# Queries and keys on two column halves and a first image projected between products, in place of a rearranged tail

## The chip, the core and the metric

The kernel runs on one core of one Trainium2 chip. The metric is the device time of one execution in microseconds. Time before the change: 3698.84 us, the median of three runs (3698.0 to 3699.41). The span in the profile, from the first to the last instruction, is 3696.3 us; the granted TensorE clock averages 0.994.

## The reference, cut to what matters

```python
# layer 0: attention over the 4096 pixels of each of 4 images, 256 channels, 32 for q and k
x = inputs.reshape(B, N, Cin)                 # B, N = 4, 4096
q = x @ Wq + bq;  k = x @ Wk + bk             # 32 columns each
v = x @ Wv + bv                               # 256 columns
attn = softmax(einsum('bnd,bmd->bnm', q, k))
x = gamma * einsum('bnm,bmc->bnc', attn, v) + inputs
# layer 1: depthwise 3x3 convolution to 768 channels, two pointwise products, a residual ...
perceived = depthwise_conv3x3(x, w_perc) + b_perc          # 256 -> 3*256
hid = gelu(w_up1 . perceived + b_up1)                      # 768 -> 512
h = x + w_up2 . hid + b_up2                                # 512 -> 256
# ... and attention of each pixel over its 3x3 neighbourhood
out = h + local_attention(h, w_qkv, b_qkv)
```

All of it is fp32.

## The kernel before

The image is cut into blocks of 512 pixels: 8 blocks an image, 32 slots in all. In slot `s` block `s` goes through the softmax's weights and products of layer 0. Between them stand the convolution of block `s - 2` on VectorE (`perceive`), the pointwise products of block `s - 3` (`hidden`, `update`, `local_values`) and the local attention of block `s - 5`. When the slots are over, a tail finishes the last blocks.

Projections. `staged[s]` holds x of block `s`; `wqk2` holds the 64 columns of queries and keys twice, to make 128:

```python
def project_qk(s):
    xc = staged[s]
    ps = bank("m", f"qk_{s}")                                  # one of 2 PSUM banks
    for kin in range(CH):                                      # CH = 2 halves of 256 channels
        nc.tensor.matmul(ps, lhsT=wqk2[:, kin]..., rhs=xc[:, kin, :], start=..., stop=...)
    st = tile_of([P, NB], "st", f"st_{s}")                     # 1 buffer
    nc.scalar.activation(st, ps, AF.Identity, bias=bqk2)
    keys[s] = tile_of([P, P], "ka", f"ka_{s}", NBLK + 1)
    for j in range(GRP):                                       # 4 key groups to 4 row quarters
        nc.sync.dma_start(out=keys[s][j * CQK : (j + 1) * CQK, :], in_=st[CQK : 2 * CQK, bass.ts(j, P)])
    nc.sync.dma_start(out=packed[:, bass.ts(s, NB)], in_=st[:CQK, :])   # queries to DRAM

def project_v(s, pair): ...            # 4 matmuls of 256 columns, bias on VectorE; two calls a block
def spread_queries(s): ...             # four copies of block s's queries from DRAM to the 4 row quarters (qa)
def energy(s, G): ...                  # four matmuls with 32 rows each, on four row quarters (L221)
def weight(s, G, half): ...            # exponential on ScalarE
def product(s, G, half): ...           # four matmuls into acc (L240)
```

The start: all eight blocks of the first image are projected ahead of the first energy.

```python
for s in range(2):
    fetch(s)                           # x of a block: two loads of 256 KB on SyncE's queue
# ... wv, bv, gam and all weights of layer 1 are loaded on ScalarE's queue ...
for s in range(NBLK):
    for job in projections(s):         # qk, v, v
        job()
    if s + 2 < NBLK:
        fetch(s + 2)
spread_queries(0)
energy(0, 0); weight(0, 0, 0); weight(0, 0, 1)
```

For images 2 to 4 the projections stand in the last slot of the image before: one block's jobs after every second product.

The convolution on VectorE: for each of 6 channel groups a first tap on ScalarE and 8 steps on VectorE (L320), in `perceive(s, parts)`; a part may be fewer rows than a block, and for the last two blocks the next part's first tap is given out one part ahead. The tail before:

```python
# in slot 31, from the 5th point on:
extra = perceive(30, [(i, 0, RB - 1) for i in range(NPC // 2)])    # 7 of 8 rows, 3 of 6 groups
# after slot 31:
turns[:] = ["m", "e", "acc", "m", "acc"]                            # PSUM banks in turn
conv = chain(perceive(30, [(i, RB - 1, RB) for i in range(NPC // 2)] + whole[NPC // 2 :]),
             perceive(31, whole))
for k in range(29, 32):
    ...                                # hid with 6 steps after each, other jobs with 0, 1, 2 or 3;
                                       # local attention of k - 2 and, already begun, of k - 1
```

For the last two blocks VectorE takes over what GpSimd does for the others: the multiplication by `near`, the local sum, and the last addition, which goes to a tile of its own:

```python
engine = nc.vector if s >= NSLOT - 2 else nc.gpsimd
...
o = tile_of([P, NB], "lo", f"lo_{s}_{c}", 2)
nc.vector.tensor_tensor(o, ps, lrdens[s], ALU.mult)
watch(o)                               # GpSimd adds it to `watched`
engine, res = nc.gpsimd, o
if s >= NSLOT - 2:
    engine, res = nc.vector, tile_of([P, NB], "o", f"res_{s}_{c}", 2)
engine.tensor_tensor(rv, ov, pixels(s, c), ALU.add)
nc.sync.dma_start(out=out[b, :, c, bass.ts(g, NB)], in_=res)
```

`hidden` is L339, `update` L365 with its `h` on VectorE L371, `guide` L439, `local_values` L479, `scores` L516, `border` L462, `local_denominator` L571 with its reciprocal L573, `local_product` L582.

Of the kernel before, what the change touches and what calls it, by code (L numbers as in the profile page):

```python
# [27 lines left out]
KR, KW = 4, W // 2  # L28
QW = KW + 1
# [15 lines left out]
def attention_then_perception_kernel(  # L45
# [34 lines left out]
    def unshifted():  # L80
# [14 lines left out]
        def job_bank(name):  # L95
            turns.append(turns.pop(0))
            if turns[-1] == "e":
                return psum.tile([P, GRP, NB], F32, tag="e", name=name, bufs=1)[:, 0, :]
            return bank(turns[-1], name)

        wqk2 = pool.tile([P, CH, 2, 2, CQK], F32, tag="wqk2", name="wqk2")
        bqk2 = pool.tile([P, 1], F32, tag="bqk2", name="bqk2")
        for r in range(2):
            nc.scalar.dma_start(out=wqk2[:, :, r], in_=w_qk)
            for s in range(2):
                at = (2 * r + s) * CQK
                nc.scalar.dma_start(out=bqk2[at : at + CQK, :], in_=b_qk[:, s : s + 1])
# [39 lines left out]
        def fetch(s):  # L149
            b, g = divmod(s, NBLK)  # L150
            staged[s] = tile_of([P, CH, NB], "xc", f"xc_{s}", 2)
            rows = x[b].rearrange("p c (h w) -> p c h w", w=WP)
            for c in range(CH):
                nc.sync.dma_start(
                    out=staged[s][:, c, :].rearrange("p (h w) -> p h w", w=W),
                    in_=rows[:, c, 1 + g * RB : 1 + (g + 1) * RB, 1 : 1 + W],
                )

        def project_qk(s):
            xc = staged[s]  # L160
            ps = bank("m", f"qk_{s}")
            for kin in range(CH):
                nc.tensor.matmul(  # L163
                    ps, lhsT=wqk2[:, kin].rearrange("p r s d -> p (r s d)"),
                    rhs=xc[:, kin, :], start=(kin == 0), stop=(kin == CH - 1),
                )
            st = tile_of([P, NB], "st", f"st_{s}")
            nc.scalar.activation(st, ps, AF.Identity, bias=bqk2)
            keys[s] = tile_of([P, P], "ka", f"ka_{s}", NBLK + 1)
            for j in range(GRP):  # L170
                nc.sync.dma_start(  # L171
                    out=keys[s][j * CQK : (j + 1) * CQK, :],
                    in_=st[CQK : 2 * CQK, bass.ts(j, P)],
                )
            nc.sync.dma_start(out=packed[:, bass.ts(s, NB)], in_=st[:CQK, :])
# [20 lines left out]
        def projections(s):  # L196
            return [
                lambda: project_qk(s),
                lambda: project_v(s, 0),
                lambda: project_v(s, 1),  # L200
            ]
# [82 lines left out]
        HALO = KR // 2  # L284
# [6 lines left out]
        def perceive(s, parts):  # L291

            g = s % NBLK
            ahead = s >= NSLOT - LAG_PERC
            percs.setdefault(s, {})

            def first(i, r0, r1):
                if i not in percs[s]:
                    if not ahead:
                        perc = tile_of([P, NB], "perc", f"perc_{s}_{i}", NPERC)  # L300
                    else:

                        if i % 2 == 0:
                            percs[s, i] = spare(f"perc_{s}_{i}")
                        perc = percs[s, i - i % 2][:, i % 2, :]
                    percs[s][i] = perc
                tap_of(i, r0, r1, 0)

            def tap_of(i, r0, r1, tap):
                half, j = divmod(i, MULT)  # L310
                dy, dx = divmod(tap, 3)
                acc = percs[s][i].rearrange("p (h w) -> p h w", w=W)[:, r0:r1, :]
                win = xv[:, half, g * RB + dy + r0 : g * RB + dy + r1, dx : dx + W]
                wt = wperc[:, half, j, tap : tap + 1]
                if tap == 0:
                    nc.scalar.activation(  # L316
                        acc, win, AF.Identity, bias=bperc[:, half, j : j + 1], scale=wt
                    )
                else:
                    nc.vector.scalar_tensor_tensor(acc, win, wt, acc, ALU.mult, ALU.add)  # L320

            for n, part in enumerate(parts):
                if n == 0 or not ahead:
                    first(*part)
                if ahead and n + 1 < len(parts):
                    first(*parts[n + 1])
                for tap in range(1, TAPS):
                    tap_of(*part, tap)
                    if part[2] - part[1] > 1 or tap % 4 == 0:
                        yield  # L330

        whole = [(i, 0, RB) for i in range(NPC)]
# [177 lines left out]
        def scores(s, half):  # L510
# [19 lines left out]
            engine = nc.vector if s >= NSLOT - 2 else nc.gpsimd  # L530
            engine.tensor_tensor(  # L531
# [8 lines left out]
        def local_sum(s):  # L540
# [5 lines left out]
            engine = nc.vector if s >= NSLOT - 2 else nc.gpsimd  # L546
            engine.memset(t, 0.0)
            for half in range(2):
                for _, rows, at in pieces(s):
                    to = tv[:, rows, columns(half)]  # L550
                    p = near_ws[s, half][:, at].rearrange("p (h w) -> p h w", w=QW)
                    engine.tensor_tensor(to, to, p, ALU.add)
# [23 lines left out]
        def local_product(s, c):  # L576
# [14 lines left out]
            engine, res = nc.gpsimd, o  # L591
            if s >= NSLOT - 2:
                engine, res = nc.vector, tile_of([P, NB], "o", f"res_{s}_{c}", 2)
            ov, rv = (t.rearrange("p (h a w) -> p h a w", a=2, w=KW) for t in (o, res))
            engine.tensor_tensor(rv, ov, pixels(s, c), ALU.add)
            nc.sync.dma_start(out=out[b, :, c, bass.ts(g, NB)], in_=res)
# [22 lines left out]
        for s in range(2):  # L619
            fetch(s)  # L620
        wv = loaded(w_v, "wv")
        bv = loaded(b_v.partition_broadcast(P), "bv", [P, C])
        gam = loaded(gamma.partition_broadcast(P), "gam", [P, 1])
        wperc = loaded(w_perc, "wperc")
# [9 lines left out]

        for s in range(NBLK):
            for job in projections(s):
                job()
            if s + 2 < NBLK:
                fetch(s + 2)
        spread_queries(0)  # L640
        energy(0, 0)
        weight(0, 0, 0)
        weight(0, 0, 1)
        points = 2 * NG
        for slot in range(NSLOT):
# [19 lines left out]
            conv = perceive(slot - LAG_PERC, whole) if slot >= LAG_PERC else iter(())  # L665
            n_steps, stepped = NPC * (TAPS - 1), 0
            extra, begun = iter(()), 4
            if slot == NSLOT - 1:

                extra = perceive(slot - 1, [(i, 0, RB - 1) for i in range(NPC // 2)])  # L670
            done = 0
            for point in range(points):
# [25 lines left out]
                while stepped < min(n_steps, -(-(point + 1) * n_steps // (points - 2))):  # L698
                    next(conv, None)
                    stepped += 1  # L700
                    if point >= begun and stepped % 3:
                        next(extra, None)
                if nxt and half == 1:
                    for job in nxt[G]:
                        job()
                    if G + 2 < NBLK:
                        fetch(slot + 1 + G + 2)
            for _ in chain(conv, extra):
                pass
# [3 lines left out]
        turns[:] = ["m", "e", "acc", "m", "acc"]  # L713
        conv = chain(
            perceive(
                NSLOT - 2,
                [(i, RB - 1, RB) for i in range(NPC // 2)] + whole[NPC // 2 :],
            ),
            perceive(NSLOT - 1, whole),
        )  # L720

        def run(*jobs):
            for job, steps in jobs:
                job()
                for _ in range(steps):
                    next(conv, None)

        last = NSLOT - 1
        for k in range(NSLOT - LAG_HID, NSLOT):
            hid, upd, new = hidden_jobs(k)  # L730
            g0, g1, s0, s1, bd, ls, ld, l0, l1 = attention_jobs(k - 2)
            hid = [(job, 6) for job in hid]
            if k == last:
                for _ in conv:
                    pass
            if k == NSLOT - LAG_HID:
                run(
                    (g0, 1), hid[0], (g1, 1), hid[1], (s0, 1), hid[2], (s1, 1), (bd, 0), (ls, 0),
                    hid[3], (upd[0], 3), (ld, 0), (upd[1], 2),
                )  # L740
            else:
                run(
                    hid[0], (ld, 0), hid[1], (l0, 1), hid[2], (l1, 1), hid[3],
                    (upd[0], 3), (upd[1], 2),
                )
            g0, g1, s0, s1, bd, ls = attention_jobs(k - 1)[:6]
            run((g0, 1), (g1, 1))
            if k == NSLOT - LAG_HID:
                run((l0, 1), (l1, 1))
            run(*((job, 1) for job in new), (s0, 1), (s1, 1), (bd, 0), (ls, 0))  # L750
        ld, l0, l1 = attention_jobs(last - 1)[6:]
        att = attention_jobs(last)
        below(NSLOT)
        local_values(NSLOT, 0)
        for job in (*att[:2], ld, *att[2:6], l0, l1, *att[6:]):
            job()

        test = [tile_of([P, NB], "o", f"test_{i}", 2) for i in range(2)]
        nc.vector.tensor_scalar(test[0], watched, -WATCH_MAX, None, ALU.is_ge)
        nc.vector.scalar_tensor_tensor(  # L760
            test[1], watched, WATCH_MAX, test[0], ALU.is_le, ALU.mult
        )
        good = tile_of([P, 1], "good", "good")
# [400 lines left out]
```

## Time and profile before

| | |
|---|---|
| time, median of 3 | 3698.84 us |
| span of the profile | 3696.3 us |
| first energy, first product | 56.2 us, 63.5 us |
| end of slot 0 (its denominator on TensorE) | 128.1 us |
| denominator of slot 31 | 3508.05 us |
| last comparison | 3688.85 us |
| matmul records of products / hid / e / qk | 4096 / 1536 / 2048 / 128 |

Each row of a timeline or of a group gives the engine, the line of the kernel, the operation, the tiles as out<-in, and a count. Matmul lengths overlap because the engine is pipelined: where records follow closely, the distance from start to start is what each costs. What stands in brackets is the time the engine sat idle before the row and what ended it. A logical fp32 matmul appears as two records. PE is TensorE, PEld its weight loads, DVE VectorE, ACT ScalarE, POOL GpSimd, SP SyncE; a q after the name is the engine's instruction queue.

### The profile page before, as it was taken

Reading aid. Unit: us, or ns where it says so; the run is one execution under the profiler, and the core shown is the slowest. Engines: PE = TensorE matmul, PEld = TensorE weight load, DVE = VectorE, ACT = ScalarE, POOL = GpSimd, SP = SyncE. Lnnn points to the kernel's source line nnn. Section 1 sums busy time; section 2 is a strip of 40 time slices with the busy share of each in tenths; the row PEclk is TensorE's granted clock in tenths of the full one; section 3 lists DMA queues with packets and bytes.
Section 4 is the critical chain, followed back from the end, with each engine's and each line's share of the span. In section 5 each row is a group of like instructions: output and inputs, shape, how many; then the busy total and the mean of one; then the engine's idle time right before and its main releaser. Section 6 shows DMA issues by size and latency. Waiting matters only on the chain.

```text
span 3696.3 us, 29966 instructions
## 1 busy us (share of the span) xinstructions
PE 3642.3 (99%) x11598; PEld 1741.6 (47%) x11598; DVE 2451.4 (66%) x2716; ACT 1166.2 (32%) x1302; POOL 744.9 (20%) x735
## 2 busy tenths in 40 slices
PE   8999999999999999999999999999999999999997
PEld 4334444454444444455444444445544444444445
DVE  2376656756677776666666777765676666777794
ACT  1223333223333333332333333333233333333231
POOL 1000012111212222112212222221122212222242
PEclk9999999999999999999999999999999999999999
DMA  4000000110000000021000000001100000000000
GB/s 108 15 18 9 3 0 15 37 39 11 15 15 15 15 15 4 11 45 42 15 1 15 15 15 15 15 19 37 32 15 15 3 12 15 15 15 12 6 12 19
DMA packets 101592, 69.05 MB, mean 19 GB/s; under 512 B 74432, under 2 KB 79552, under 8 KB 101312
## 3 DMA queue, kind: packets, MB, share of 16 engines
q1 hardware_dynamic: 98304, 63.47, 6.6%
q10 hardware_dynamic: 3136, 3.58, 0.3%
q8 instruction: 93, 1.52, 0.2%
q14 instruction: 59, 0.48, 0.0%
HBM read 46.04 MB, written 18.87 MB: 18 GB/s over the span
## 4 chain that ended last, share of the span: by engine, by line
PE 94%; DVE 3%; DMA 1%; POOL 1%; SPq 0%; issue 0%; ACT 0%; ACTq 0%; DVEq 0%; POOLq 0%
PE acc L240 47%; PE hid L339 18%; PE e L221 7%; PE dx L365 6%; PE lv L479 3%; PE g L439 3%; PE lo L582 2%; PE s L516 2%; PE v L184 2%; DVE perc L320 2%; PE qk L163 1%; PE dps L263 1%; PE ld L571 1%; SPq L171 0%; DMA packed<-st 0%; DVE lrden L573 0%
## 5 line engine op out<-in xcount | busy, mean ns | idle before, releaser
L240 PE MATMUL acc<-p,v 128*128 128x512 f32 x4096 | 1841.5, 595 | 3.2 <-DVE o L269 3.2
L320 DVE SCALAR_TENSOR_TENSOR perc<-xp,wperc,perc 128x512 f32<-128x512 f32 (+2 forms) x1560 | 1315.6, 849 | 624.3 <-ACT perc L316 590.3
L240 PEld LDWEIGHTS acc<-p,v 128*128 128x128 f32 x4096 | 769.9, 191 | 915.2 <-issue 901.4
L229 ACT ACTIVATE p<-e 128x1024 f32<-128x1024 f32 x512 | 524.4, 1024 | 1573.5 <-PE e L221 744.6
L339 PE MATMUL hid<-perc,wup 128*128 128x512 f32 x1536 | 694.1, 601 | 0.0
L254 DVE TENSOR_TENSOR den<-den,p 128x1024 f32<-128x1024 f32 x480 | 594.2, 1238 | 74.2 <-ACT p L229 68.2
L339 PEld LDWEIGHTS hid<-perc,wup 128*128 128x128 f32 x1536 | 282.5, 190 | 398.1 <-issue 390.9
L531 POOL TENSOR_TENSOR lp<-lp,near 128x396 f32<-128x396 f32 x60 | 87.0, 1452 | 1352.4 <-ACT lp L529 1352.4
L221 PE MATMUL e<-qa,ka 32*128 32x512 f32 x2048 | 295.0, 642 | 5.1 <-DMA qa<-packed 3.1
L365 PE MATMUL dx<-hid,wup 128*128 128x512 f32 x512 | 235.9, 604 | 0.0
L229 ACT ACT_TABLE_LOAD x116 | 148.8, 1283 | 233.8 <-issue 119.2
L343 ACT ACTIVATE hid<-hid,bup 128x512 f32<-128x512 f32 x128 | 88.0, 687 | 397.7 <-PE hid L339 397.7
L265 DVE RECIPROCAL rden<-dps 128x512 f32<-128x512 f32 x32 | 107.4, 3358 | 118.0 <-PE dps L263 118.0
L371 DVE SCALAR_TENSOR_TENSOR h<-dx,bup,xp 128x256 f32<-128x256 f32 x128 | 55.9, 478 | 187.4 <-PE dx L365 187.4
L143 POOL TENSOR_TENSOR watched<-watched,lrden 128x512 f32<-128x512 f32 x32 | 62.3, 1948 | 527.9 <-DVE lrden L573 527.9
L143 POOL TENSOR_TENSOR watched<-watched,lo 128x512 f32<-128x512 f32 x64 | 131.2, 2051 | 181.1 <-DVE lo L589 174.8
L221 PEld LDWEIGHTS e<-qa,ka 32*128 32x128 f32 x2048 | 81.0, 183 | 173.8 <-issue 162.9
L343 ACT ACT_TABLE_LOAD x121 | 155.2, 1283 | 11.9 <-PE hid L339 9.7
L365 PEld LDWEIGHTS dx<-hid,wup 128*128 128x128 f32 x512 | 92.5, 189 | 138.7 <-issue 114.8
L316 ACT ACTIVATE perc<-xp,bperc,wperc 128x512 f32<-128x512 f32 (+2 forms) x195 | 154.9, 798 | 0.0
L143 POOL TENSOR_TENSOR watched<-watched,den 128x512 f32<-128x512 f32 x32 | 40.6, 1269 | 507.0 <-DVE den L256 507.0
L189 DVE TENSOR_TENSOR v<-v,bv 128x512 f32<-128x512 f32 x64 | 44.0, 691 | 130.9 <-PE v L184 130.6
(87 smaller groups left out, 2227.7 us busy)
## 6 DMA issues: line engine op xcount, KB each, us to landing
xp<-in_x SPq DMA_DIRECT2D x32, 528.0 KB, 4.7
xc<-in_x SPq DMA_DIRECT2D x64, 256.0 KB, 3.9
out<-lo SPq DMA_DIRECT2D x60, 256.0 KB, 2.0
qa<-packed SPq DMA_DIRECT2D x128, 64.0 KB, 3.7
ka<-st SPq DMA_DIRECT2D x128, 16.0 KB, 1.8
packed<-st SPq DMA_DIRECT2D x32, 64.0 KB, 1.9
wup<-in_w_up ACTq DMA_DIRECT2D x1, 1536.0 KB, 7.3
out<-res SPq DMA_DIRECT2D x4, 256.0 KB, 2.0
```

Source lines behind the costliest of these rows:

```text
L143: nc.gpsimd.tensor_tensor(watched, watched, values, ALU.add)
L221: nc.tensor.matmul(e[:, j, :], lhsT=key[rows, :], rhs=queries[s][rows, :], start=True, stop=True,)
L229: nc.scalar.activation(p, energies[s, G][:, 2 * half : 2 * half + 2, :], AF.Exp)
L240: nc.tensor.matmul(accs[s][c], lhsT=v[:, 2 * half + i, bass.ts(c, P)], rhs=p[:, i, :], start=(first and i == 0), stop=(G == NG - 1 and hal ...
L254: nc.vector.tensor_tensor(den, den, p, ALU.add)
L316: nc.scalar.activation(acc, win, AF.Identity, bias=bperc[:, half, j : j + 1], scale=wt)
L320: nc.vector.scalar_tensor_tensor(acc, win, wt, acc, ALU.mult, ALU.add)
L339: nc.tensor.matmul(ps, lhsT=wup1[:, i, bass.ts(d, P)], rhs=percs[s][i], start=(i == 0), stop=(i == NPC - 1),)
L343: nc.scalar.activation(hids[s][:, d, :], ps, AF.Gelu, bias=bup1[:, d : d + 1])
L365: nc.tensor.matmul(ps, lhsT=wup2[:, d, bass.ts(c, P)], rhs=hids[s][:, d, :], start=(d == 0), stop=(d == NHC - 1),)
L439: nc.tensor.matmul(ps, lhsT=wg[:, kin, bass.ts(i, P)], rhs=pixels(s, kin), start=(kin == 0), stop=(kin == CH - 1),)
L479: nc.tensor.matmul(ps[:, half * C : (half + 1) * C], lhsT=keys_of(s, t, half, kin), rhs=wlv[:, kin, :], start=(kin == 0), stop=(kin == CH ...
```

## The change

It has three parts.

1. Queries and keys of two blocks are computed at once: block `s` on the lower 64 columns of TensorE, block `s + 1` on the upper 64. This is to replace the doubled columns by useful ones.
2. The first image's projections mostly move between the products of slot 0, as those of the other images stand already; x of blocks 2 to 7 is loaded at the start on ScalarE's queue, into buffers that are free at that time, and the weights of layer 1 are loaded after that. This is to let the products begin sooner.
3. The tail is another: the convolution is done block by block with four steps after each job, no part of it stands in slot 31, and GpSimd does its usual work for the last two blocks as well, except the last addition, which VectorE does in place.

```diff
-        wqk2 = pool.tile([P, CH, 2, 2, CQK], F32, tag="wqk2", name="wqk2")
+        wqk = pool.tile([P, CH, 2, CQK], F32, tag="wqk", name="wqk")
         def fetch(s):
-            staged[s] = tile_of([P, CH, NB], "xc", f"xc_{s}", 2)
+            # blocks 2..7 of the first image: in "hid", "h" and "lq" buffers; others as before
+            queue = nc.scalar if 2 <= s < NBLK else nc.sync
         def project_qk(s):
             for kin in range(CH):
-                nc.tensor.matmul(
-                    ps, lhsT=wqk2[:, kin].rearrange("p r s d -> p (r s d)"),
-                    rhs=xc[:, kin, :], start=(kin == 0), stop=(kin == CH - 1),
-                )
+                for r in range(2):
+                    nc.tensor.matmul(
+                        ps[2 * r * CQK : 2 * (r + 1) * CQK, :],
+                        lhsT=wqk[:, kin].rearrange("p s d -> p (s d)"),
+                        rhs=staged[s + r][:, kin, :], start=(kin == 0), stop=(kin == CH - 1),
+                    )
             # one activation to st; then packed and ka of block s, and of block s + 1
         def projections(s):
+            pair = [lambda: project_qk(s)] if s % 2 == 0 else []
+            return pair + [lambda: project_v(s, 0), lambda: project_v(s, 1)]
 ...
+        for s in range(NBLK):
+            fetch(s)
         gam = loaded(gamma.partition_broadcast(P), "gam", [P, 1])
+        first = {s: projections(s) for s in range(NBLK)}
+        first[0].pop(0)()
+        spread_queries(0)
         # the weights of layer 1 are loaded here
-        for s in range(NBLK):
-            for job in projections(s):
-                job()
-            if s + 2 < NBLK:
-                fetch(s + 2)
-        spread_queries(0)
+        for job in first[0] + first[1]:
+            job()
+        first[2].pop(0)()
         energy(0, 0)
         weight(0, 0, 0)
         weight(0, 0, 1)
+        first = [first[4][:1] + first[2], first[3], first[6][:1] + first[4][1:], first[5], first[6][1:], first[7]]
 ...
+            if slot == 0:
+                nxt = first + [[]] * (NG - len(first))
-            if slot == NSLOT - 1:
-                extra = perceive(slot - 1, [(i, 0, RB - 1) for i in range(NPC // 2)])
 ...
-            engine = nc.vector if s >= NSLOT - 2 else nc.gpsimd      # near, local sum
+            nc.gpsimd. ...
-            if s >= NSLOT - 2:
-                engine, res = nc.vector, tile_of([P, NB], "o", f"res_{s}_{c}", 2)
+            last = nc.vector if s >= NSLOT - 2 else nc.gpsimd
+            last.tensor_tensor(ov, ov, pixels(s, c), ALU.add)
 ...
-        turns[:] = ["m", "e", "acc", "m", "acc"]
-        # (the loop of the tail before)
+        turns.append("acc")
         for k in range(NSLOT - LAG_HID, NSLOT):
             hid, upd, new = hidden_jobs(k)
+            att = attention_jobs(k - LAG_ATT + LAG_HID)
+            ahead = k + LAG_HID - LAG_PERC
+            conv = perceive(ahead) if ahead < NSLOT else iter(())
+            for job in (
+                att[0], hid[0], att[1], hid[1], att[2], hid[2], att[3], att[4], att[5],
+                hid[3], att[6], *upd, att[7], att[8], *new,
+            ):
+                job()
+                for _ in range(4):
+                    next(conv, None)
+        att, last = (attention_jobs(a) for a in (NSLOT - 2, NSLOT - 1))
         below(NSLOT)
         local_values(NSLOT, 0)
-        for job in (*att[:2], ld, *att[2:6], l0, l1, *att[6:]):
+        for job in (*att[:6], *last[:6], att[6], last[6], *att[7:], *last[7:]):
             job()
```

`attention_jobs` gives guide, guide, scores, scores, border, local sum, local denominator, product, product. The final test of `watched` is written with four VectorE operations instead of three.

## The prediction

> **What bounds the kernel now.** I read the page first: busy shares, then the chain of waits.
>
> ```profile
> PE 3642.3 (99%) x11598; PEld 1741.6 (47%) x11598; DVE 2451.4 (66%) x2716; ACT 1166.2 (32%) x1302; POOL 744.9 (20%) x735
> ...
> PE 94%; DVE 3%; DMA 1%; POOL 1%; SPq 0%; issue 0%; ACT 0%; ACTq 0%; DVEq 0%; POOLq 0%
> ```
>
> TensorE is busy nearly throughout and carries 94% of the chain. So in the middle of the run a microsecond of TensorE removed is a microsecond of time, and work moved to other engines is free. The 3% of VectorE and 1% of DMA must lie where TensorE waits, so I asked for TensorE's timeline at both ends, and at one slot that projects the next image.
>
> The slot first. The columns are start, length, engine, line, operation, count; a logical fp32 matmul is two records, and the distance between starts is its cost on the path.
>
> ```profile
> 704.87 1.88 PE L163 MATMUL qk<-xc,wqk 128*128 128x512 f32 x4
> 706.59 3.62 PE L184 MATMUL v<-wv,xc 128*128 128x256 f32 x16
> 710.13 1.14 PE L221 MATMUL e<-qa,ka 32*128 32x512 f32 x8
> 711.21 5.42 PE L339 MATMUL hid<-perc,wup 128*128 128x512 f32 x12
> ```
>
> One block's queries and keys cost 706.59 - 704.87 = 1.72 us, its values 3.54 us, one group of four energies 1.08 us, and nothing waits in between.
>
> The start:
>
> ```profile
> 49.53 3.62 PE L184 MATMUL v<-wv,xc 128*128 128x256 f32 x16
> 56.23 3.23 PE L221 MATMUL e<-qa,ka 32*128 32x512 f32 x8 [3.08 <-DMA qa<-packed]
> 61.49 2.09 PE L221 MATMUL e<-qa,ka 32*128 32x512 f32 x8 [2.03 <-ACT p L229]
> 63.51 7.79 PE L240 MATMUL acc<-p,v 128*128 128x512 f32 x16
> ...
> 128.09 1.02 PE L263 MATMUL dps<-den,ones 128*128 128x512 f32 x2
> ```
>
> The first product starts at 63.5 us, after all eight blocks of projections and two bare waits; slot 0 then takes 128.1 - 63.5 = 64.6 us without a gap. The projections before it are worth 8 x (1.72 + 3.5) = about 42 us, so some 21 us of these 63.5 are filling and waiting. SyncE and ScalarE say what the filling is made of:
>
> ```profile
> 0.81 5.62 SPq L154 DMA_DIRECT2D xc<-in_x  x4
> 18.66 0.69 ACT L168 ACTIVATE st<-qk,bqk 128x512 f32<-128x512 f32 x1 [5.27 <-DMA packed<-st]
> ```
>
> Four quarter-megabyte loads of x took 5.6 us to issue, 1.4 us each, though the same pair takes 1.02 us later, when nothing else is in flight: issuing is held back while the transfers crowd. And `st` has one buffer, so its next writing waits for the copies out of it.
>
> The end:
>
> ```profile
> 3508.05 1.25 PE L263 MATMUL dps<-den,ones 128*128 128x512 f32 x2 [2.16 <-DVE den L256]
> ...
> 3572.33 2.07 PE L571 MATMUL ld<-lsum,ones 128*128 128x512 f32 x2 [6.46 <-POOL lsum L557]
> 3574.19 6.81 PE L339 MATMUL hid<-perc,wup 128*128 128x512 f32 x12
> ...
> 3688.10 0.56 PE L766 MATMUL good_sum<-good,ones 128*128 128x1 f32 x2 [6.53 <-DVE good L764]
> ```
>
> The tail lasts from 3509 to 3688.9 us (the last comparison), 180 us, and 7.4 us of the span follow it. Its TensorE work, by starts, is 42 us for each of three blocks (hid 20.6, dx 6.9, g 3.4, s 3.1, lo 3.1, lv 3.5, ld 0.9, border 0.3) and 11 us for each of two more blocks of local attention: 150 us. So the present tail is already within 30 us of TensorE's own work.
>
> **What the skill says.** The Trainium skill's "TensorE: Matmul & The Clock Gate", section "Part 3: Packing small matmuls", says that matmuls on different row or column tiles of the array run at once, and gives 2.38x for three column tiles. The trace agrees for row tiles: the records of four energies start 7 ns apart, and the group costs 1.08 us where four matmuls of that length in a row would cost 3.4 us. No run here has column tiles yet. "TensorEngine Tiling (Array Packing)", section "Tiling Modes", says that a change of tiling mode drains the array. The trace fits: from a product's last record to the first energy record pass 0.52 us, against 0.43 between two products. "DMA: Bandwidth & Descriptors", section "Issuing engines are not separate DMA queues", says that loads issued by ScalarE share the engines with SyncE's; so twelve loads moved to ScalarE's queue should not arrive sooner. No trace before tests this. The clock-gate page's Part 1 says that an idle array drops to half clock: after the 6.46 us wait above, twelve records of hid took 6.81 us instead of 5.42.
>
> **Part 1: queries and keys of two blocks at once.** Before, the 128 columns held the 64 wanted ones twice; a pair of blocks costs 2 x 1.72 = 3.44 us. After, four logical matmuls of 64 columns stand on two halves. If the halves overlap as rows do, four half-steps of 0.43 us remain, with about 0.1 us for each that the energies also lose (0.53 instead of 0.43 from pass to pass): 1.8 to 2.2 us, I take 2.1. Gain 1.34 us a pair, 5.4 us an image. For images 2 to 4 this lies wholly on TensorE's path: **-16 us**. The halved count of `st` activations (0.69 us each) is off the path.
>
> **Part 2: the first image.** Only queries and keys of blocks 0 to 3 and values of 0 and 1 stay ahead of the first product; 6 x 3.5 + 2 x 2.1 = 25 us move into slot 0. The slot then ends at (first product) + 64.6 + 25. For the first product: x of blocks 0 and 1 has landed at about 9 us (issued by 6.4, and 3 us or more to landing). But ScalarE now issues twelve more loads of x before its first `st`, and at 1.4 us each (they meet the same crowd) it comes free at about 19 to 21 us, against 11.4 before. The `st` ends at 21 to 22; SyncE then issues ten copies and four of `qa` at about 0.58 us each, 8 us, and the last lands 2 to 3 us later: energies at about 32, exponentials, first product at about 35 (estimates from those rows). The slot ends at 124 to 125 instead of 128.1. Were ScalarE not held up, the product would start near 29 and the gain be 10. I take **-5 us**, which holds the first image's share of Part 1.
>
> **Part 3: the old tail.** It drops three things: half of one block's convolution inside slot 31, the unbroken row of convolution steps, and VectorE doing GpSimd's work for the last two blocks. Each job is followed by four steps, so 40 steps stand before the local denominator's reciprocal, and the next block's `lv` follows the last `h`. A step takes 0.86 us (1315.6 us over 1560 is 0.84, more when GpSimd works alongside).
> - Block 29: VectorE leaves slot 31 at 3517.5. 40 x 0.86 + 3.4 (reciprocal) + 4 x 0.86 + 0.9 (`h`) + 4 x 0.86 + 0.9 = 46.4, so 3564, and 3568 after `lv`.
> - Block 30: 1 us to start, 3 us of waiting for first taps that ScalarE holds behind its TensorE results (estimate), 46.4, `lv` 3.5: 3622.
> - Block 31 has no steps: 27.6 us of TensorE to the last hid, 4.3 for the local sum (9.8 us from scores to denominator at 3542.5, of which 5.5 are covered), then 0.9 + 6.9 + 3.1 + 3.5, and 1 us of cold clock: 3669.
> - The last two attentions: values 1.7, twice (3.4 + 3.1 + 0.3 + 1.2 waiting): 3687. GpSimd needs about 8 more for the second sum: 3695. Denominator and reciprocal 5: 3700. Then four results in turn, each product 0.7, watched by GpSimd 1.5 (the addition in place must wait for that), added 0.8: 3712. Test and end 4: 3716, plus the 7.4: 3723 against 3696.3.
>
> That is **+27 us**. Sum: -16 - 5 + 27 = +6, so 3698.8 + 6 = **3705 us**.
>
> **The rivals.** (a) Column halves don't overlap: two streams of 128 rows each must be read at once, which row tiles never asked. Then Part 1 brings nothing and the time is about 3724. The skill's table speaks against it; no record here does. (b) The tail costs much less, because VectorE still has slack: in it only blocks 29 and 30 exceed TensorE's 42 us, and 0.77 us a step (seen where GpSimd is idle) saves 4 us in each. With a smoother end the tail is +15 and the time 3692. For it: the before tail's own gaps; against it: VectorE is the chain from 3465 to 3556 even now. (c) The start gains its full 10 to 12 us, with the others as predicted: 3699. (d) The start becomes DMA-bound, as weights and x crowd the small copies: the first product at 42 us, 3712.
>
> **Range and chances.** Part 1 may lie between 0 and -18, Part 2 between +2 and -12, Part 3 between +15 and +38; they are independent, so 8 times in 10 the sum lies between -11 and +25: 3688 to 3724. Two per cent is 74 us, beyond any of these: within 2% is nearly certain.
>
> **What would show it.** qk at slot 7: about 2.1 us to the next start for every second block, four records of 64 columns in pairs some ns apart; 3.4 us would prove rival (a). The first L240 near 35 us and slot 0's dps near 125. ScalarE's first `st` after 19 us, or near 12 if issue isn't held. In the tail: dps to dps shows slot 31 unchanged at 107.7 us, `lv` of blocks 29 and 30 waiting for VectorE, spacing about 54 us, and the last four results with GpSimd between VectorE's steps. The prediction is wrong if the tail grows under 15 us or the start loses time.

## The result and the profile after

The changed kernel takes 3712.92 us (median of six runs, 3710.0 to 3714.57) against 3698.7: a ratio of 1.0037, with a 95% interval of 1.0024 to 1.005. It is 14 us slower; 3705 was predicted, in a range of 3688 to 3724. In the two profiles the spans differ by 3707.9 - 3696.3 = 11.6 us, and all that follows divides these.

The page of the changed kernel, its busy shares and its chain:

```profile
PE 3629.5 (98%) x11598; PEld 1726.9 (47%) x11598; DVE 2434.1 (66%) x2676; ACT 1159.9 (31%) x1287; POOL 750.1 (20%) x753
...
PE 95%; DVE 2%; DMA 1%; POOL 1%; issue 0%; ACTq 0%; ACT 0%; SPq 0%; POOLq 0%; DVEq 0%
```

TensorE's busy time went down by 12.8 us and the span went up: the loss lies where TensorE waits. In the rows that follow, `qk` and `v` are the projections of layer 0, `e` its energies, `acc` its products and `dps` the denominator that ends a slot; `ld`, `lv` and `lo` are denominator, values and products of the local attention. TensorE's timeline in slot 7, where the second image is projected:

```profile
707.48 3.60 PE L253 MATMUL acc<-p,v 128*128 128x512 f32 x8
711.01 1.94 PE L176 MATMUL qk<-xc,wqk 128*64 128x512 f32 x8
712.88 3.72 PE L200 MATMUL v<-wv,xc 128*128 128x256 f32 x16
716.53 1.14 PE L234 MATMUL e<-qa,ka 32*128 32x512 f32 x8
...
809.12 1.81 PE L576 MATMUL lo<-lp,lv 128*128 128x99 f32 x12 [1.08 <-DVE v L205]
```

Two blocks' queries and keys take 712.88 - 711.01 = 1.87 us. They are eight records of 64 columns now, in the time of little more than four. The last row is a wait that the slot did not have before. The start, TensorE first, then ScalarE and SyncE:

```profile
26.24 1.94 PE L176 MATMUL qk<-xc,wqk 128*64 128x512 f32 x8 [0.78 <-DVE v L205]
35.47 3.13 PE L234 MATMUL e<-qa,ka 32*128 32x512 f32 x8 [7.29 <-DMA qa<-packed]
40.63 2.09 PE L234 MATMUL e<-qa,ka 32*128 32x512 f32 x8 [2.03 <-ACT p L242]
42.65 7.67 PE L253 MATMUL acc<-p,v 128*128 128x512 f32 x16
...
131.96 1.02 PE L276 MATMUL dps<-den,ones 128*128 128x512 f32 x2
```

```profile
5.00 15.38 ACTq L166 DMA_DIRECT2D xc<-in_x  x12
21.60 1.28 ACT L182 ACT_TABLE_LOAD   x1 [21.60 <-DMA xc<-in_x]
22.89 0.69 ACT L182 ACTIVATE st<-qk,bqk 128x512 f32<-128x512 f32 x1
...
26.70 0.58 SPq L186 DMA_DIRECT2D packed<-st  x1
29.57 2.42 SPq L188 DMA_DIRECT2D ka<-st  x4
```

The first product starts 21 us sooner than before, but 25 us of projections moved behind it, so slot 0 ends at 131.96, which is 3.9 us later. ScalarE spends 15.38 us issuing the loads of x and reaches its first `st` at 22.89 us. The issue goes at the pace of the transfers: the DMA engines move about 217 GB/s in this time, and at this rate twelve loads of 256 KB take 14.5 us (an estimate). The tail:

```profile
3498.78 1.02 PE L276 MATMUL dps<-den,ones 128*128 128x512 f32 x2
...
3536.23 2.08 PE L565 MATMUL ld<-lsum,ones 128*128 128x512 f32 x2 [4.19 <-POOL lsum L551]
3538.09 9.19 PE L361 MATMUL dx<-hid,wup 128*128 128x512 f32 x16
...
3554.48 3.29 PE L475 MATMUL lv<-wlv,h 128*128 128x256 f32 x14 [2.66 <-DVE h L367]
...
3701.00 0.56 PE L727 MATMUL good_sum<-good,ones 128*128 128x2 f32 x2 [9.99 <-DVE good L725]
```

In each of blocks 29 and 30 TensorE waits in two places: for GpSimd's local sum ahead of `ld`, and for VectorE's `h` ahead of `lv`. After the first of these waits the clock granted to TensorE is half for a while (a mean of 0.76 from 3538.1 to 3547.1), and the sixteen records of dx take 9.19 us; without a wait they take 7.03.

From denominator to denominator on TensorE's timeline, and from the last of them to the end of the span:

| stretch, us | before | after | difference |
|---|---|---|---|
| start to the end of slot 0 | 128.09 | 131.96 | +3.9 |
| slot 1 | 80.63 | 82.81 | +2.2 |
| slots 7, 15 and 23, together | 447.2 | 434.2 | -13.0 |
| slot 31 | 108.76 | 106.43 | -2.3 |
| tail | 188.25 | 209.12 | +20.9 |
| all other slots | | | 0.0 |

Unrounded, the sum is 11.6 us. Slot 1 has the same instructions in both kernels; what its 2.2 us are is said with the last experiment.

### The profile page after: what moved, and what is told of

Read it like the earlier page. It is cut to its first block, busy times and chain, and to the rows that moved or that the text cites. A ratio compares the mean times of both kernels' runs of the same rounds, so it can differ in the third digit from the quotient of the medians.

```text
span 3707.9 us, 29852 instructions
## 1 busy us (share of the span) xinstructions
PE 3629.5 (98%) x11598; PEld 1726.9 (47%) x11598; DVE 2434.1 (66%) x2676; ACT 1159.9 (31%) x1287; POOL 750.1 (20%) x753
## 4 chain that ended last, share of the span: by engine, by line
PE 95%; DVE 2%; DMA 1%; POOL 1%; issue 0%; ACTq 0%; ACT 0%; SPq 0%; POOLq 0%; DVEq 0%
PE acc L253 48%; PE hid L335 18%; PE e L234 7%; PE dx L361 6%; PE lv L475 3%; PE g L435 3%; PE s L512 3%; PE v L200 3%; PE lo L576 2%; DVE perc L327 1%; PE dps L276 1%; PE ld L565 1%; PE qk L176 1%; DVE lrden L567 1%; ACTq L166 0%
## 5 line engine op out<-in xcount | busy, mean ns | idle before, releaser
L327 DVE SCALAR_TENSOR_TENSOR perc<-xp,wperc,perc 128x512 f32<-128x512 f32 x1536 | 1305.9, 854 | 635.8 <-ACT perc L323 600.9
L323 ACT ACTIVATE perc<-xp,bperc,wperc 128x512 f32<-128x512 f32 x192 | 154.4, 804 | 0.0
```

Of the source, the lines that this page charges most:

```text
L323: nc.scalar.activation(acc, win, AF.Identity, bias=bperc[:, half, j : j + 1], scale=wt)
```

## The experiments

All start from the kernel before, and each was run beside it. The edits of the start are shown against Parts 1 and 2 together, those of the halves against Part 1 alone, the last one against the run in which ScalarE is not held. "Slot 0" below is the time at which it ends.

**Part 1 alone.**

```diff
-                nc.tensor.matmul(ps, lhsT=wqk2[:, kin]..., rhs=xc[:, kin, :], ...)
+                for r in range(2):
+                    nc.tensor.matmul(ps[64 * r : 64 * (r + 1), :], lhsT=wqk[:, kin]..., rhs=staged[s + r][:, kin, :], ...)
```

> The kernel before with Part 1 alone: two blocks' queries and keys on two column halves; the start keeps its order (all eight blocks of the first image ahead of the first energy) and the tail is that of before. Theory (overlapping halves are worth on the path what the slots 7, 15 and 23 of the changed kernel show, 4.33 us each): 13.0 us for images 2 to 4, and up to 4 more in the first image, so 3682 to 3686 us. Rival (the saving in the first image is swallowed by the copies out of the single buffer of st, which already hold ScalarE back there): 13 and no more, 3686. Rival (what slots 7, 15, 23 show comes from something else in the change): under 8 us, above 3690.

Measured: 3699.45 us against 3700.45, ratio 0.9999 (0.9991 to 1.0008): nothing. The theory's number and the first rival's failed. The last rival's number held (above 3690), but not its reason: slots 7, 15 and 23 did fall by 4.33 us each with Part 1 alone. It is slot 0 that ended at 142.43 instead of 128.09. Its TensorE timeline says why:

```profile
37.75 1.04 PE L165 MATMUL qk<-xc,wqk 128*64 128x512 f32 x2 [3.24 <-DMA xc<-in_x]
40.06 3.40 PE L165 MATMUL qk<-xc,wqk 128*64 128x512 f32 x6 [1.26 <-DMA xc<-in_x]
```

A pair needs both its blocks of x ahead of its first matmul. With two buffers neither load can start before the pair ahead has been used up, and on SyncE's queue both stand behind ten copies of queries and keys (from 12.36 to 19.20 us for the first pair). So TensorE waits at every pair, and the 13.0 us of the later images are lost again in 14.3 us of slot 0. Part 2 isn't an extra to Part 1: with the start and the two buffers of before, Part 1 is worth nothing.

**Parts 1 and 2**, with the tail of before.

> Parts 1 and 2 with the tail of before: the changed kernel but for its tail. Theory (the start loses although it was meant to win; the end of slot 0 comes 3.9 us later than before in the profile although queries and keys of the first image also cost less): slower than halves_only by 4 to 10 us, 3688 to 3694. Rival (the loss seen at the start is the chance of one profile): equal to halves_only or faster by up to 5 us, 3679 to 3685.

Measured: 3690.57 us, ratio 0.9975 (0.9966 to 0.9985). The time is in the range written for the first theory, but the comparison in it failed: this is 9 us faster than Part 1 alone, not slower, because Part 1 alone loses the start. Slot 0 ends at 134.07 here. The first two parts together win 10 us.

**Part 3 alone.**

> The kernel before with Part 3 alone: no convolution in slot 31, four steps after each job, GpSimd for the last two blocks. Theory (the parts add up: from the denominator of slot 31 to the end 20.9 us more, slot 31 itself 2.3 us less): 3698.7 + 18.6 = 3717 us. Rival (the changed kernel's tail is dearer than this by itself because of what stands ahead of it): 3710 or less. The prediction said +27, 3726.

Measured: 3719.81 us against 3700.45, ratio 1.0057 (1.0043 to 1.007). Its tail is 210.89 us and its slot 31 106.43, so the two together grew by 20.3; in the changed kernel by 18.5. In these two stretches the parts add up to within 2 us, and Part 3 is what makes the change slower. By the medians they add up less well: -9.9 for Parts 1 and 2 and +19.4 here make 9.5 us, where the whole change cost 14.2.

**The loads of x after the first st.**

```diff
-        for s in range(NBLK):
+        for s in range(2):
             fetch(s)
         ...
         first[0].pop(0)()          # queries and keys of blocks 0 and 1, with st
+        for s in range(2, NBLK):
+            fetch(s)
```

> As halves_and_start, but ScalarE issues the twelve loads of x of blocks 2 to 7 after its first st instead of ahead of it; everything else is the same, the weights of layer 1 follow the loads. Theory (ScalarE held for 15.4 us by issuing these loads is the loss): st at about 12 us instead of 22.9, first product near 32 instead of 42.7, end of slot 0 near 122, in all about 10 us less than halves_and_start. Rival (the crowd on the DMA engines delays the small copies of queries and keys wherever the loads stand): st is early but the copies land late, first product at 38 or later, at most 4 us less than halves_and_start.

Measured: 3685.61 us, ratio 0.9961 (0.9947 to 0.9975), 5 us under the run before it where 10 was expected. The theory was half of it: slot 0 ended at 128.98, not near 122. ScalarE's timeline:

```profile
11.35 0.69 ACT L186 ACTIVATE st<-qk,bqk 128x512 f32<-128x512 f32 x1 [3.83 <-PE qk L180]
11.35 16.29 ACTq L170 DMA_DIRECT2D xc<-in_x  x12
...
34.06 1.93 ACT L246 ACTIVATE p<-e 128x1024 f32<-128x1024 f32 x2
```

`st` is early, the copies land in time although x is being loaded beside them, and the first energies start at 21.45 us. So the rival falls. But ScalarE now issues x for 16.29 us and then the weights, and reaches the exponentials only at 34.06. The hold had been moved, not removed.

**ScalarE not held.**

```diff
-            queue = nc.scalar if 2 <= s < NBLK else nc.sync
+            queue = nc.sync            # blocks 0 to 3 at once, 4 to 7 after the copies of 2 and 3
-        wperc = loaded(w_perc, "wperc")      # and the other weights
+        wperc = loaded_later(w_perc, "wperc")
         ...
                 product(slot, G, half)
+                if later:
+                    later.pop(0)()     # one load of a weight after each product of slot 0
```

> As halves_and_start (tail of before), but ScalarE issues no load of x and, until slot 0 runs, no weights of layer 1: SyncE loads x of blocks 0 to 3 at once and 4 to 7 after the copies of blocks 2 and 3, and the weights are issued one by one between the exponentials of slot 0. Theory (what remained in x_loads_after_st is ScalarE held for 21.4 us between its first st and its first exponential by issuing loads; the energies were ready there at 21.5 us): first product at about 28 us instead of 38.1, end of slot 0 at about 118 instead of 129.0, in all about 10 us under x_loads_after_st, 3675 us. Rival (the crowd of x on the DMA engines moves into the slot and makes projections wait for x there): first product early, but slot 0 longer than 90.9 us, total 3682 or more.

```profile
22.62 1.14 PE L238 MATMUL e<-qa,ka 32*128 32x512 f32 x8
25.90 2.09 PE L238 MATMUL e<-qa,ka 32*128 32x512 f32 x8 [2.13 <-ACT p L246]
27.92 7.78 PE L257 MATMUL acc<-p,v 128*128 128x512 f32 x16
...
117.47 1.02 PE L280 MATMUL dps<-den,ones 128*128 128x512 f32 x2
```

Measured: 3673.3 us, ratio 0.9927 (0.9914 to 0.9941). First product at 27.92, slot 0 at 117.47, and 89.6 us between them, so the projections inside the slot wait for nothing. The theory holds with its numbers; the rival falls.

**The weights later, x as in the change.** All nine issues of weights stand after `weight(0, 0, 1)`.

> As halves_and_start, but the weights of layer 1 are issued after the first two exponentials instead of after the first st; the twelve loads of x stay ahead of st. Theory (two causes add up at the start: ScalarE held by x up to 22.9 us, and the copies of queries and keys, 5.9 us to landing for the first, crowded by the weights issued beside them): st stays at 23, the copies land in 2 to 3 us each, energies at about 32 instead of 36.3, first product at about 39 instead of 43.7, in all 4 us less than halves_and_start: 3686. Rival (the weights are no matter, the copies are slow by themselves): 3690.

```profile
23.41 0.69 ACT L186 ACTIVATE st<-qk,bqk 128x512 f32<-128x512 f32 x1
32.46 3.31 PE L238 MATMUL e<-qa,ka 32*128 32x512 f32 x8 [3.59 <-DMA qa<-packed]
```

Measured: 3688.37 us, ratio 0.9967 (0.9954 to 0.998). First product at 39.82, slot 0 at 129.34. From `st` to the energies 12.6 us pass in the changed kernel and 13.6 in Parts 1 and 2, here 9.0; SyncE issues its ten copies without the gap that stands above before 29.57. So the weights cost 3.5 to 4.5 us by holding up the copies, beside what the x loads cost. Slot 0 ended 4.7 us sooner than in Parts 1 and 2, but the total moved by 2.2 us instead of 4: slot 1 took 83.0 us in this profile against 80.6.

**GpSimd for the last two blocks**, in the order of before.

```diff
-            engine = nc.vector if s >= NSLOT - 2 else nc.gpsimd     # near; local sum
+            engine = nc.gpsimd
-            # VectorE's last addition goes to a tile `res`
+            # VectorE's last addition is done in place
```

> The kernel before, but GpSimd does the multiplication by near and the local sum for the last two blocks too, and the last addition is done in place by VectorE, as in the changed kernel; the order of the tail and the half convolution in slot 31 stay as before. Theory (of the old tail's 21 us, the last stretch after the last lv is one part): from the denominator of slot 31 to the end about 8 us more than 188.2: 196, total 3707. Rival (the engines are no matter, the order of jobs and steps is all): within 2 us of before.

Measured: 3700.84 us against 3699.4, ratio 1.0001 (0.9993 to 1.001). The tail is 190.0, 1.8 us more. The theory falls.

**No half convolution in slot 31.**

```diff
-                extra = perceive(slot - 1, [(i, 0, RB - 1) for i in range(NPC // 2)])
+                pass
-                [(i, RB - 1, RB) for i in range(NPC // 2)] + whole[NPC // 2 :],
+                whole,
```

> The kernel before with no convolution of block 30 in slot 31; the unbroken row of steps, the order of jobs and VectorE's part for the last two blocks stay. Theory (VectorE carries the tail up to block 31, and the half was 24 steps of 0.83 us, against 24 single-row steps of 0.3 us that go away): slot 31 at 106.4 us instead of 108.8, tail up by 20 - 7 = 13 us from 188.2 to 201, total about 3709. Rival (the order of jobs is what costs in the old tail): tail within 3 us of 188.

Measured: 3705.9 us against 3699.6, ratio 1.0018 (1.0011 to 1.0024). Slot 31 is 106.43, the tail 196.67. TensorE's timeline shows where it is paid:

```profile
3611.51 2.08 PE L339 MATMUL hid<-perc,wup 128*128 128x512 f32 x2 [5.57 <-DVE perc L320]
3618.70 2.07 PE L339 MATMUL hid<-perc,wup 128*128 128x512 f32 x2 [5.11 <-DVE perc L320]
```

Block 31's first hid now waits for VectorE's convolution. The half is worth 8.4 us of tail, for 2.3 us in slot 31. Moving VectorE's work, 13 us by the estimate above, cost 8.4, so part of it was slack.

**The old order with VectorE's part kept.**

> As old_tail_only, but VectorE does its part for the last two blocks (near, local sum, last addition to a tile of its own), as in the kernel before. In the order of before this part was worth only 1.8 us of tail (gpsimd_last). Theory (in the old order both last blocks' sums stand at the very end, one after the other, and nothing covers them): tail 203 instead of 210.9, total about 3712. Rival (worth 2 us here too): tail 209.

Measured: 3716.06 us, ratio 1.0047 (1.0032 to 1.0062). Tail 208.88, slot 31 106.43. The engines are worth 2.0 us here too: the rival holds. The old tail's 20.3 us thus divide into 6.1 for the half (8.4 - 2.3), 2.0 for the engines, and 315.3 - 303.1 = 12.2 for the rest, where 315.3 and 303.1 are slot 31 and tail together in this run and the one before it. The rest is the order of jobs and steps together with the PSUM banks in turn, the first taps given out one part ahead and the test with one operation less; no run takes these apart. The first taps are in sight: in the tail of this run VectorE waits 6.9 us for ScalarE's first taps, in the one before it 0.7 us.

**The order of the two halves.**

```diff
-            for kin in range(CH):
-                for r in range(2):
+            for r in range(2):
+                for kin in range(CH):
                     nc.tensor.matmul(...)
```

> As halves_only, but both matmuls of the lower half of the columns stand before both of the upper half, instead of alternating; the same work. Theory (neighbouring matmuls on different halves overlap, those on the same half don't): the pair costs much more than 1.87 us, between 2.6 (one pass overlaps at the border) and 3.4 (none). Rival (narrow matmuls are cheap by themselves, whatever their order): 1.9 us again.

The order is no matter; the theory falls:

```profile
715.48 1.94 PE L165 MATMUL qk<-xc,wqk 128*64 128x512 f32 x8
717.36 3.72 PE L189 MATMUL v<-wv,xc 128*128 128x256 f32 x16
```

1.88 us, as in the change. In the trace the eight records still start in pairs, 13 ns apart here, 7 ns in the change. The second record of the first pair waits for the load of the other block, so it is the upper half's first matmul: it starts 13 ns after the lower half's first and 0.48 us ahead of the lower half's second, which stands before it in the kernel.

**Both blocks on the same half.**

```diff
-                        ps[64 * r : 64 * (r + 1), :], ...      # one bank
+                        ps[:64, :], ...                        # r = 0 and 1: a bank each
```

> As halves_only, but both blocks of a pair stand on the lower 64 columns, each in a PSUM bank of its own (two activations to st instead of one); as many matmuls of 64 columns as there. The order of the matmuls turned out not to matter in halves_in_turn, so this tells the two remaining readings apart. Theory (matmuls on different halves run at once, whatever their order within the group): on one half they follow one another, 8 records at 0.43 us, 3.4 us for a pair instead of 1.87, and slots 7, 15 and 23 are at 149 us as before. Rival (a matmul of 64 columns is itself cheaper): 1.9 us again.

```profile
707.16 3.65 PE L167 MATMUL qk<-xc,wqk 128*64 128x512 f32 x8
710.73 3.72 PE L193 MATMUL v<-wv,xc 128*128 128x256 f32 x16
```

3.57 us for a pair, and slots 7, 15 and 23 at 151.6, where 3.4 and 149 were expected. It isn't the narrowness: the gain is the overlap of two halves, 3.57 to 1.87, and it doesn't depend on which matmul stands next to which within the group.

**A version that beats both, and slot 1.** Slot 1 took from 78.8 to 83.0 us in these profiles with the same instructions.

```diff
-                nc.scalar.dma_start(out=w, in_=w_qkv[:, :, i * C : (i + 1) * C])   # in slot 1
+        # the same two loads, in slot 0 after the weights
```

> As start_unheld, and the two loads of layer 1's query and key weights that slot 1 waits for (3.3 us each) are issued in slot 0, after the other weights. Theory (these two waits bring TensorE to half clock or not, by chance, which is why slot 1 took between 79.0 and 83.0 us in the runs so far): slot 1 at about 72 us (79.0 less 6.7), total 7 to 11 us under start_unheld, 3664. Rival (the matmuls wait for the tile copies behind them as long as for the loads): 3 us at most.

```profile
119.96 0.66 PE L412 MATMUL wq_turning<-ident,wq_in 128*128 128x128 f32 x4
123.20 5.40 PE L257 MATMUL acc<-p,v 128*128 128x512 f32 x8 [2.57 <-DVE o L286]
```

Measured: 3668.34 us against 3699.6, ratio 0.9916 (0.9903 to 0.993), 5 us under the unheld start where 7 to 11 were expected. The waits for loads are gone, but behind the first stood another: the products wait 2.57 us for VectorE to empty the last slot's accumulators, and eight records then take 5.40 us instead of 3.60. Slot 1 takes 75.08, where about 72 was expected.

The spread of slot 1 is the clock, and the profiles of the other runs show it. In all 13 of them TensorE waits 6.3 to 6.7 us in slot 1, nearly the same, but the granted clock is not. A row gives the stretch and its length, TensorE's busy time and records, the mean granted clock, and what the DMA engines did. Slot 1 of the loads of x after the first `st`, of Parts 1 and 2, of Part 1 alone, and of the changed kernel:

```profile
128.98:208.04 79.06, 72.49 (x232) 0.98 0.06 17
134.07:214.70 80.63, 74.00 (x231) 0.96 0.06 17
142.43:224.23 81.80, 75.32 (x231) 0.94 0.06 17
131.96:214.77 82.81, 76.22 (x232) 0.92 0.06 17
```

The clock is half for one, two, three or four stretches of 3.4 us. Four of the 13 profiles have a mean of 0.98 and take 78.8 to 79.2 us, five have 0.96 (80.5 to 80.9), one 0.94, three 0.92 (82.8 to 83.0). In the last version it is 0.98, and the slot is shorter by what TensorE no longer waits: 2.57 us instead of some 6.6. So 4 us of the slot are the edit's, and the other 3.7 us between its profile and that of the unheld start are the clock's. What decides between 0.98 and 0.92 no run shows.

## Why the prediction was right

The time fell into the range, and the signs of two of the three parts were right, but the three sizes were off and partly made up for each other, which was luck: -16, -5 and +27 were predicted, and the profiles show -13.0, +3.9 (slot 0) and +18.5 (slot 31 and tail), with 2.2 of slot 1, which no part makes. By the prediction's own sign, "wrong if ... the start loses time", Part 2 was wrong, and it lies outside its range of +2 to -12.

- **Part 1.** The mechanism was right, by the two runs on halves; rival (a) is dead. A pair costs 1.87 us, and the product ahead of it and the values behind it each take 0.1 us more (3.53 and 3.65 against 3.43 and 3.54): 2.08 us in all, where 2.1 was taken. Yet an image gains 4.33 us and not 5.4. The missing term is one wait of 1.08 us for VectorE, new in slot 7 and as long in slots 15 and 23: 4 x (3.44 - 2.08) - 1.1 = 4.3. `lo` takes the PSUM bank that a block's values have just left, and VectorE comes to these values only after four steps of the convolution; before, that block's own queries and keys (1.72 us) stood between and hid it. The run with both blocks on one half has the same 1.08 us. That makes 13.0 in place of 16.
- **Part 2.** The step that failed is the first product at "about 35". ScalarE was free of the loads of x at 20.4, as worked out, but `st`, put to end at "21 to 22", ended at 23.6: the issue of `gam` (1.15 us) and a table load (1.28 us) stand ahead of it. The copies, put at 10 to 11 us from there, took 11.9, with the weights in their way; and from the energies to the first product I took 3 us where 7.2 pass. The rows shown for the kernel before have it: 56.23 to 63.51, because the second energy waits for both exponentials and stands ahead of the product. Half clock is in both: here the mean granted clock is 0.50 from 33.5 to 43.8, and with ScalarE not held, at 0.80, the same way takes 5.3 us. After the first product, 89.3 us to the end of the slot were measured and 64.6 + 25 predicted. The sign of -5 was therefore wrong for the part as built. Rival (d) named the first product at 42 us and 3712 in all, which is what came, and was right in part: the weights hold up the copies by 3.5 to 4.5 us (the run with the weights later), the loads of x do not (energies at 21.45 with x loaded beside the copies), and the time from the energies to the product is no matter of DMA. That Part 1 alone gains nothing, so that Part 2 is worth 9 us beside it (3699.45 to 3690.57) and 26 with ScalarE free (to 3673.3), no step of mine said.
- **Part 3.** The blocks were right one by one: from the denominator of slot 31 to block 30's first guide 58.8 us (60 predicted), then 54.7 (54), 45.3 (47), and 50.3 to the end (54). The last is short in small pieces: GpSimd's second sum came 6.4 us after TensorE's work and not 8, and 6.0 us of the span follow the last comparison, not 7.4. Rival (b)'s faster steps explain little: block 31's 48 steps in the changed kernel took 40.1 us, 0.84 each where I took 0.86. What I left out is slot 31: I showed its 2.16 us wait for VectorE and didn't count that it goes away, writing that the slot would stay at 107.7 (it is 108.76 before and 106.43 after).
- The profile's difference is 11.6 us and that of the medians 14.2. Both profiles are of the fastest run of their kernel (3698.0 and 3710.0). The clock in slot 1 alone makes up to 4 us between runs; whether that is the rest stays open.

"DMA: Bandwidth & Descriptors" of the Trainium skill, in "Issuing engines are not separate DMA queues", says that the time saved on the sequencer by issuing elsewhere is usually small beside the transfer. Here it was not small: twelve loads took 15.4 to 16.3 us of ScalarE, as long as moving them took, and ScalarE's next instruction waited behind them.

## What to carry to other kernels

An engine that issues a row of large loads does nothing else meanwhile: put such loads where nothing urgent stands behind them in the engine's order (here on SyncE, ahead of its copies and after them), and count the issue time on the path of whatever does stand behind them. Packing two small matmuls side by side pays on the path, but what it needs (both inputs at once) can cost as much as it wins if buffers and loads stay as they were, and TensorE's time saved can uncover a wait that this time had hidden. And when a wait goes away, look at the same row for the one that ended just before it.

## What the runs showed of the hardware

- Two fp32 matmuls of 64 columns on different column halves, with different moving data of 128 rows each, overlap almost wholly: four of them cost 1.87 us on two halves and 3.57 us on one. The order in which they are given within the group makes no difference (1.88): given one half after the other, the upper half's first started 13 ns after the lower half's first.
- Twelve loads of 256 KB in runs of 256 bytes took ScalarE 15.4 to 16.3 us to issue, one behind the other; eight took SyncE 9.8 us at the start and 8.0 in slot 0 (ScalarE not held), and two 1.02 us with little else in flight.
- After some of TensorE's waits its granted clock is half for one or more stretches of 3.4 us, and its records lengthen: eight product records took 5.40 us instead of 3.60 after a wait of 2.57 us, sixteen dx records 9.19 instead of 7.03 after one of 4.19. It does not follow every such wait: after 2.66 us ahead of `lv` (3554.48 in the changed kernel) the clock stayed whole and fourteen records took 3.29 us.
